# Attention block of a fused four-layer kernel: row pairs share tiles, the layer norm's scale and shift move to GpSimd, and the order of the row-pair loop is rewritten

## The chip, the core and the metric

The kernel runs on one core of one Trainium2 chip. The metric is device time in microseconds (us) from launch to the last output. Lower is better. All data are fp32.

An engine is named as the profile names it: PE is the matrix engine (TensorE), PEld its weight loads, DVE the vector engine, ACT the scalar engine, POOL is GpSimd, and SP is the engine that issues most of the transfers.

## The reference, cut to what matters

The input `x` is an image of 256 by 256 pixels with 128 channels. Four residual layers follow each other; the change touches layer 0 alone. Layer 0 normalises `x` by groups, then by a layer norm over the channels, and runs attention along each image row with a bias that all rows share:

```python
zn = (z - mu) * rsqrt(var + EPS) * ln_scale + ln_bias      # z: group-normalised x
q, k, v = (zn @ Wq), (zn @ Wk), (zn @ Wv)                  # 4 heads of 32 channels
bias = zn @ Wb                                             # one number per pixel and head
g = sigmoid(zn @ Wg)
scores = einsum('bijhd,bikhd->bijkh', q, k) / sqrt(32) + bias[:, None]
a = softmax(scores, axis=-2)                               # over the 256 columns k of row i
o = g * einsum('bijkh,bikhd->bijhd', a, v)
x = x + o @ Wo
```

The other three layers (a gated recurrence over a spectrum, a triangle product, a convolution) are the same in both kernels.

## The kernel before

Channels lie on the 128 partitions and pixels along the free axis. The whole program is unrolled. The stages run one after the other: `transpose_in` (the image is transposed to channel-major form and its group statistics are taken), then `attention`, `recurrence`, `triangle` and `convolution`. Each engine works through its own queue in order; a tile's readers and writers are tied by semaphores, and a pool hands out a fixed number of buffers per name, so that the next user of a buffer waits for the last reader of the one before. `pin` keeps the instructions in the order in which the code emits them.

**Weights.** `attention_weights` folds the layer norm's `ln_scale` into every projection matrix and its `ln_bias` into a bias column per projection (`wb["q"]`, `wb["k"]`, `wb["gn"]`, `vb` for v, `wb["4"]` for the pair bias). So the stored `zn` is the centred and scaled value alone, and each projection adds its bias where it is read out of PSUM. `bounded` computes a bound on the scores; if it is small enough, as in these runs, `attend_bounded` is taken, which needs no maximum in the softmax. Otherwise `attend_any` would be.

**Norm stage** (inside `attention`): 64 blocks of 1024 pixels. For each block PE centres the pixels (`zc`), ACT squares them (`sq`), DVE copies them out (`zs`), PE averages the squares (`var`), ACT takes a logarithm and an exponential (`rs`), and DVE multiplies (`zn`). `pair_bias` runs once per two blocks, two blocks late: PE multiplies `zn` by the bias weights (`pbias`), DVE copies the result out (`bi`), POOL's queue stores `zn` in DRAM (`znT`, L352), and SP's queue stores the bias.

**Attention loop** (`attend_bounded`, L620 to L646): 128 row pairs `rp`, with rows `a = 2 rp` and `b = 2 rp + 1`. The steps, with the names that the profile shows:

- `project` (two pairs ahead): PE makes q, k, v, g for 512 pixels (`ppq`, `ppk`, `ppv`, `ppg`). ACT reads q, k and g out, DVE reads v out (`tv`). These four and the output `px` share two PSUM buffers under the tag `pj`.
- `score` (one pair ahead): PE makes a row's scores for four heads (`sc`), two heads to a PSUM buffer, two buffers in all.
- `biased`: DVE adds the shared bias `bT` to two heads at once (`e`, 128 x 1024), and `exponent`: ACT takes the exponential in place.
- `fold`: DVE adds the two halves of the columns (`es`), so that the softmax's denominator needs half the matmuls.
- `values`: PE makes numerator and denominator of one row in one PSUM tile (`nd`, one bank, two buffers).
- `gated`: DVE multiplies the denominator by `1 + exp(-g)` (`dn`); `inverse`: ACT takes a logarithm and an exponential of it; `divide`: DVE multiplies the numerator by it (`og`).
- `output`: PE applies Wo (`px`), DVE adds the residual row (`x`); `squares`: ACT takes the statistics for the next layer (`junk`).

Instructions are issued through helpers, so the profile gives the helper's line: L60 for every matmul, L54 for an activation, L308 for the vector work of the norm stage, L477 for that of the attention loop. The tile names tell them apart.

The PSUM memory is full: four banks of `sc`, two of `pj`, two of `nd`.

Of the kernel before, what the change touches and what calls it, by code (L numbers as in the profile page):

```python
# [9 lines left out]
F32 = mybir.dt.float32  # L10
AF = mybir.ActivationFunctionType
# [6 lines left out]
P = 128  # L18
# [12 lines left out]
class Kernel:  # L31
# [186 lines left out]
    def attention_weights(self, wp):  # L218

        nc, tc, I = self.nc, self.tc, self.i  # L220
        with self.pool(name="awp", bufs=1, space=PSUM) as ps0:
            def load(src, name):
                t = wp.tile(list(src.shape), F32, name=name)
                nc.scalar.dma_start(t, src)
                return t
            lns, lnb = (load(I["L0_conv_ln_" + n].rearrange("(c o) -> c o", o=1), "ln" + n[0]) for n in ("scale", "bias"))
            w, wb, raws = {}, {}, {}

            for nm, f in (("q", -1.0 / math.sqrt(HD)), ("k", 1.0), ("v", 1.0), ("g", 1.0), ("b", -1.0)):
                raw = raws[nm] = load(I["L0_conv_W" + nm], "raw" + nm)  # L230
                m = raw.shape[1]
                pb = ps0.tile([P, 2], F32, name="pb" + nm, tag="gn")
                self.mm(pb[:m, 0:1], raw, lnb)
                wb[nm] = wp.tile([m, 1], F32, name="wb" + nm)
                nc.vector.tensor_scalar_mul(wb[nm], pb[:m, 0:1], 0.5 if nm == "g" else f)
                w[nm] = wp.tile([P, m], F32, name="w" + nm)
                nc.vector.tensor_scalar(w[nm], raw, lns, f, ALU.mult, ALU.mult)
            wb["gn"] = wp.tile([P, 1], F32, name="wbgn")
            nc.vector.tensor_scalar_mul(wb["gn"], wb["g"], -2.0)

            vbl = wp.tile([P, P], F32, name="vbl")
            nc.vector.tensor_copy(vbl, lnb.to_broadcast([P, P]))
            pvb = ps0.tile([P, P], F32, name="pvb", tag="gn")
            self.mm(pvb, vbl, raws["v"])
            vb = wp.tile([P, P], F32, name="vb")
            nc.vector.tensor_copy(vb, pvb)
            wo = {"f": load(I["L0_conv_Wo"], "wo"), "h": wp.tile([P, P], F32, name="woh")}
            nc.vector.tensor_scalar_mul(wo["h"], wo["f"], 0.5)
            self.lnb = lnb

            wb["4"] = wp.tile([P, 1], F32, name="wbb4")
            nc.vector.memset(wb["4"], 0.0)
            for k in range(4):
                nc.vector.tensor_copy(wb["4"][32 * k:32 * k + NH], wb["b"])
            w["32"] = wp.tile([P, 32], F32, name="wb32")
            nc.vector.memset(w["32"], 0.0)
            nc.vector.tensor_copy(w["32"][:, :NH], w["b"])
        return w, wb, vb, wo, self.bounded(wp, raws, w, wb)
# [21 lines left out]
    def attention(self, wp, weights, later, xT, x1T, znT, biasD, stats0, stats1, shift1):  # L280
        nc, tc, I = self.nc, self.tc, self.i
        w, wb, vb, wo, small = weights
        with ExitStack() as c:
# [18 lines left out]
            with ExitStack() as c1:  # L302
# [4 lines left out]
                wbb, wb32 = wb["4"], w["32"]  # L307
                pin = lambda f: lambda *a, **k: tc.keep_in_program_order(f(*a, **k))  # L308
                mm, act, tt, ts = pin(self.mm), pin(self.act), pin(V.tensor_tensor), pin(V.tensor_scalar_add)
                flat = lambda t: t.rearrange("p k n -> p (k n)")  # L310
# [23 lines left out]
                def normalise(b):  # L334
# [7 lines left out]
                    tt(zn[b // 2][:, s:s + 1024], zs[b], rs, ALU.mult)  # L342

                def pair_bias(m):
# [6 lines left out]
                    ts(bi, pb, wbb)  # L351
# [27 lines left out]
            with tc.If(flag > 0) as branch:  # L379
                self.attend_bounded(xT, x1T, znT, bias, first, w, wb, vb, wo, stats1, shift1)  # L380
            self.last = {}
            with branch.Else():
                self.attend_any(xT, x1T, znT, bias, w, wb, wo, stats1, shift1)
# [70 lines left out]
    def attend_bounded(self, xT, x1T, znT, bias, first, w, wb, vb, wo, stats1, shift1):  # L454
# [4 lines left out]
        with ExitStack() as c:  # L459
# [20 lines left out]
            loaded, t, e, es, nd, dn, og, x1s = {0: first}, {}, {}, {}, {}, {}, {}, {}  # L480
# [14 lines left out]
            def project(rp, nm):  # L495
# [4 lines left out]
                if nm == "v":  # L500
# [3 lines left out]
                    tt(o, pv, vb.unsqueeze(1).to_broadcast([P, 4, P]), ALU.add)  # L504
                else:
                    pp = ps.tile([P, 512], F32, name="pp" + nm, tag="pj")
                    mm(pp, w[nm], z)
                    if nm == "g":

                        act_t(o, pp, AF.Exp, bias=wb["gn"], scale=-1.0)  # L510
                    else:
                        act_i(o, pp, AF.Identity, bias=wb[nm])
# [16 lines left out]
            def biased(i, p2):  # L529
                if i < N:  # L530
                    x = hp.tile([P, 2, 2, N], F32, name="e", bufs=8)
                    tt(x, e[i, p2], bT[:, 2 * p2:2 * p2 + 2], ALU.add)
                    e[i, p2] = x

            def exponent(i, p2):
                if 0 <= i < N:
                    act_t(e[i, p2], e[i, p2], AF.Exp, scale=-1.0)

            def fold(i):

                x = es[i] = hp.tile([P, NH, N], F32, name="es")
                for p2 in range(2):
                    y = e[i, p2]
                    tt(x[:, 2 * p2:2 * p2 + 2], y[:, :, 0, :], y[:, :, 1, :], ALU.add)

            def values(i):

                v, r = t[i // 2, "v"], i % 2
                nd[i] = ps.tile([P, 2, N], F32, name="nd", tag="nd")
                for kc in range(2):  # L550
                    for h in range(NH):
                        hs = slice(h * HD, (h + 1) * HD)
                        mm(nd[i][hs, 0, :], v[:, 2 * r + kc, hs], e[i, h // 2][:, h % 2, kc, :], start=kc == 0, stop=kc == 1)
                folded = i in es
                for kc in range(1 if folded else 2):
                    for h in range(NH):
                        hs = slice(h * HD, (h + 1) * HD)
                        mm(nd[i][hs, 1, :], ones, es[i][:, h] if folded else e[i, h // 2][:, h % 2, kc, :],
                           start=kc == 0, stop=folded or kc == 1)

            def gated(i):

                d = dn[i] = hp.tile([P, N], F32, name="dn")
                g = t[i // 2, "g"][:, (i % 2) * N:(i % 2 + 1) * N]
                stt(d, g, 1.0, nd[i][:, 1, :], ALU.add, ALU.mult)

            def inverse(i):
                if i >= 0:
                    act_t(dn[i], dn[i], AF.Ln)
                    act_t(dn[i], dn[i], AF.Exp, scale=-1.0)  # L570

            def divide(i):
                if i < 0:
                    return
                if i % 2 == 0:
                    og[i // 2] = pj.tile([P, 512], F32, name="og")
                rows = slice((i % 2) * N, (i % 2 + 1) * N)
                tt(og[i // 2][:, rows], nd[i][:, 0, :], dn[i], ALU.mult)
# [27 lines left out]
            for h in range(NH):  # L606
                pt = ps.tile([P, 2, 2, P], F32, name="pbt", tag="nd")
                for jc in range(2):
                    for kc in range(2):
                        tc.keep_in_program_order(  # L610
                            nc.tensor.transpose(pt[:, kc, jc, :], bias[:, jc, h, kc * P:(kc + 1) * P], self.ident))
                tc.keep_in_program_order(
                    V.tensor_copy(bT[:, h].rearrange("p k j -> p (k j)"), pt.rearrange("p k a j -> p (k a j)")))
            for i in range(2):
                score(i)
                for p2 in range(2):
                    biased(i, p2)
                    if (i, p2) != (1, 1):
                        exponent(i, p2)
            for rp in range(N // 2):  # L620
                a, b = 2 * rp, 2 * rp + 1
                score(a + 2)
                inverse(b - 2)
                biased(a + 2, 0)
                divide(a - 2)
                biased(a + 2, 1)
                divide(b - 2)
                for nm in "qkvg":
                    if nm == "g":
                        fold(a)  # L630
                        exponent(b, 1)
                        exponent(a + 2, 0)
                    project(rp + 2, nm)
                output(rp - 1)
# [3 lines left out]
                fold(b)  # L638
                biased(b + 2, 0)
                exponent(b + 2, 0)  # L640
                biased(b + 2, 1)
                values(a)
                gated(a)
                inverse(a)
                values(b)
                gated(b)  # L646
            inverse(N - 1)
            divide(N - 2)
            divide(N - 1)
# [3 lines left out]
    def attend_any(self, xT, x1T, znT, bias, w, wb, wo, stats1, shift1):  # L653

        nc, tc = self.nc, self.tc
        with ExitStack() as c:
# [7 lines left out]
            with tc.For_i(0, N // 2) as rp:  # L664
# [5 lines left out]
                self.attend(rp, zn, xr, x1, w, wb, wo["h"], bias, pj, hp, ps, parts)  # L670
# [9 lines left out]
    def attend(self, rp, zn, xr, x1, w, wb, wo, bias, pj, hp, ps, stats1):  # L680
# [4 lines left out]
        for nm in ("q", "k", "g"):  # L685
# [3 lines left out]
            if nm == "q":  # L689
                self.act(t, pp, AF.Identity, bias=wb["q"])  # L690
            elif nm == "k":
                nc.vector.tensor_scalar_add(t, pp, wb["k"])
            else:

                self.act(t, pp, AF.Tanh, bias=wb["g"], scale=0.5)
# [41 lines left out]
        nc.vector.scalar_tensor_tensor(og, po.rearrange("c r j -> c (r j)"), wb["v"], proj["g"], ALU.add, ALU.mult)  # L737
# [714 lines left out]
```

## Time and profile before

| what | value |
|---|---|
| time, median of 3 runs | 5322.12 us (5320.36 to 5322.81) |
| the profiled execution's own time | 5321.36 us |
| its span, first to last instruction | 5319.6 us |
| mean granted clock of PE | 0.977 |
| PE busy | 5079.0 us (95%) |
| DVE busy | 4210.7 us (79%) |
| ACT busy | 3655.6 us (69%) |
| POOL busy | 266.7 us (5%) |

The busy times are sums over all stages. The stages that the change touches are short parts of the span: from 0 to about 232 us the image is transposed, from about 232 to 495 us the norm stage runs, from about 495 to 1835 us the attention loop. The profile tells when an instruction ran, how long it took, and what ended the idle time of its engine before it. Two instructions of DVE or ACT that follow each other without a wait overlap a little, so a row's mean duration is more than what one more instruction adds to the engine's time. Matmul durations are modelled and overlap as well; what PE needs is read from the start of one group of matmuls to the start of the next.

### The profile page before, as it was taken

How to read it: one execution, taken by the hardware profiler on the slowest of the kernel's cores; microseconds unless marked ns; L12 is line 12 of the kernel's file. 1: busy time of each engine (PE TensorE's matmuls, PEld its weight loads, DVE VectorE, ACT ScalarE, POOL GpSimd, SP SyncE). 2: the span in 40 equal slices, each digit the busy share in tenths (PEclk: the TensorE clock that was granted, in tenths of full speed). 3: DMA queues.
4: the chain of work that ended last, by engine and by line, in shares of the span. 5: the costliest groups of instructions: out<-in, count | busy, mean ns of one | idle time of the engine just before them, and what ended most of it. 6: DMA issues, size and time to landing. Idle time of an engine off the chain costs nothing.

```text
span 5319.6 us, 76896 instructions
## 1 busy us (share of the span) xinstructions
PE 5079.0 (95%) x30069; PEld 2836.1 (53%) x30069; DVE 4210.7 (79%) x5534; ACT 3655.6 (69%) x5179; POOL 266.7 (5%) x488
## 2 busy tenths in 40 slices
PE   6699999999999899999999999899999989999999
PEld 4433555555555433333333333338999954439999
DVE  5666999999999799999999999555333536679886
ACT  4376777777777799999999999684333357763110
POOL 1100000000000000000000000000111010000000
PEclk7799999999999999999999999999999999999999
DMA  8875222222222222222222221577667678865432
GB/s 282 339 265 199 72 80 76 80 76 77 80 73 83 71 63 68 69 69 69 68 73 69 65 72 65 230 284 263 232 231 243 233 270 301 291 221 181 149 125 68
DMA packets 185930, 788.66 MB, mean 148 GB/s; under 512 B 36083, under 2 KB 39432, under 8 KB 136384
## 3 DMA queue, kind: packets, MB, share of 16 engines
q1 hardware_dynamic: 120212, 514.73, 29.6%
q0 software_dynamic: 60416, 268.46, 13.0%
q8 instruction: 240, 3.93, 0.3%
q10 hardware_dynamic: 4936, 0.50, 0.1%
q14 instruction: 126, 1.03, 0.1%
HBM read 512.28 MB, written 271.32 MB: 147 GB/s over the span
## 4 chain that ended last, share of the span: by engine, by line
PE 52%; DVE 31%; issue 12%; ACT 2%; DMA 1%; POOL 1%; POOLq 0%; ACTq 0%; SPq 0%; DVEq 0%
PE z L60 9%; PE m L60 7%; PE nd L60 6%; PE sc L60 6%; PE po L60 4%; PE zc L60 3%; DVE tr L824 3%; DVE t L821 3%; DVE y L821 3%; DVE p L821 3%; DVE yf L821 3%; PE ppv L60 3%; PE ppq L60 3%; PE px L60 3%; PE ppk L60 2%
## 5 line engine op out<-in xcount | busy, mean ns | idle before, releaser
L54 ACT ACTIVATE e<-e 128x1024 f32<-128x1024 f32 x512 | 525.5, 1052 | 166.4 <-DVE e L477 166.3
L477 DVE TENSOR_TENSOR e<-sc,bT 128x1024 f32<-128x1024 f32 x512 | 612.3, 1217 | 25.1 <-PE sc L60 25.1
L984 DVE TENSOR_TENSOR LR<-z,sg 128x512 f32<-128x512 f32 x256 | 268.5, 1049 | 364.5 <-ACT sg L54 359.7
L60 PE MATMUL m<-U,v 128*128 128x128 f32 x4608 | 516.7, 276 | 6.6 <-DVE v L1299 6.6
L60 PEld LDWEIGHTS m<-U,v 128*128 128x128 f32 x4608 | 516.5, 192 | 6.7 <-DVE v L1299 6.7
L60 PE MATMUL z<-wf,zt 128*128 128x128 f32 x4096 | 460.7, 276 | 3.6 <-DVE zn L984 3.6
L60 PEld LDWEIGHTS z<-wf,zt 128*128 128x128 f32 x4096 | 460.6, 193 | 4.6 <-DVE zn L984 4.4
L60 PE MATMUL sc<-tq,tk 32*128 32x256 f32 x4096 | 361.4, 408 | 3.3 <-DVE e L477 3.3
L54 ACT ACTIVATE sg<-z 128x512 f32<-128x512 f32 x256 | 152.8, 597 | 307.8 <-PE z L60 307.8
L60 PE MATMUL var<-sq,omat 128*128 128x512 f32 x768 | 360.8, 599 | 1.2 <-ACT rs L54 1.2
L477 DVE TENSOR_TENSOR es<-e 128x512 f32<-128x512 f32 x512 | 329.1, 684 | 0.0
L54 ACT ACTIVATE rs<-var,eps 128x1024 f32<-128x1024 f32 x192 | 213.4, 1112 | 168.1 <-PE var L60 168.1
L60 PEld LDWEIGHTS sc<-tq,tk 32*128 32x128 f32 x4096 | 220.8, 184 | 190.6 <-issue 147.9
L54 ACT ACTIVATE dn<-dn 128x256 f32<-128x256 f32 (+1 forms) x640 | 279.8, 456 | 61.6 <-DVE dn L477 51.3
L60 PE MATMUL nd<-e,tv 128*32 128x256 f32 x4096 | 271.0, 382 | 0.0
L60 PE MATMUL zc<-xin,lc 128*128 128x512 f32 x512 | 247.5, 607 | 6.1 <-DVE zn L984 5.6
L60 PEld LDWEIGHTS var<-sq,omat 128*128 128x128 f32 x768 | 137.9, 189 | 203.7 <-issue 154.6
L60 PE MATMUL av<-y,ident 128*128 128x512 f32 x384 | 193.0, 612 | 44.0 <-DVE y L821 44.0
L60 PE MATMUL po<-LR 128*128 128x256 f32 x1024 | 222.2, 380 | 7.0 <-DVE LR L984 7.0
L1336 ACT COPY m4s<-m 128x512 f32<-128x512 f32 x32 | 18.7, 585 | 285.6 <-PE m L60 285.6
L60 PEld LDWEIGHTS po<-LR 128*128 128x128 f32 x1024 | 194.1, 190 | 34.2 <-DVE LR L984 7.7
L54 ACT ACTIVATE rs<-rs 128x1024 f32<-128x1024 f32 x192 | 202.8, 1056 | 6.1
(329 smaller groups left out, 10076.7 us busy)
## 6 DMA issues: line engine op xcount, KB each, us to landing
zt<-znT SPq DMA_DIRECT2D x128, 1024.0 KB
znT<-zn POOLq DMA_DIRECT2D x64, 1024.0 KB, 5.8
xin<-x2T SPq DMA_DIRECT2D x64, 1024.0 KB
xr<-x3T SPq DMA_DIRECT2D x46, 768.0 KB
xin<-in_x_dram SPq DMA_DIRECT2D x64, 512.0 KB
xT<-xo POOLq DMA_DIRECT2D x64, 512.0 KB, 10.2
xr<-xT SPq DMA_DIRECT2D x64, 512.0 KB
xin<-xT SPq DMA_DIRECT2D x32, 1024.0 KB
```

The lines of the kernel that those rows point to most:

```text
L54: return self.nc.scalar.activation(out, in_, func, bias=bias, scale=scale, **kw)
L60: return self.nc.tensor.matmul(out, lhsT, rhs, start=start, stop=stop)
L477: pin = lambda f: lambda *a, **k: tc.keep_in_program_order(f(*a, **k))
L821: pin(V.tensor_tensor(out, a, b_, op))
L824: pin(V.scalar_tensor_tensor(out, a, k, b_, op0, op1))
L984: pin = lambda f: lambda *a, **k: tc.keep_in_program_order(f(*a, **k))
L1336: nc.scalar.copy(m4, m[4])
```

## The change

It has four parts.

1. **Scale and shift.** The projections use the raw weights (q and the pair bias with their constant factors), and all bias columns are gone. In the norm stage a new POOL instruction, one for each block of 128 x 1024, multiplies `zn` in place by `ln_scale` and adds `ln_bias`. The read-outs of q, k and g lose their bias operand.
2. **v.** It is read out of PSUM by ACT in place of DVE.
3. **Shared tiles.** The biased scores and exponentials of a row's four heads lie in one tile of 128 x 2048 (`e`, four buffers in place of eight of half the size). `fold` is one instruction for each row in place of two (the folded tile is now called `ks`). Numerators and denominators of both rows lie in one PSUM tile of two banks (`nd`, one buffer in place of two of half the size). `gated`, `inverse` and `divide` run once for each pair on 128 x 512 in place of twice on 128 x 256.
4. **Order.** In each pass of the loop the folds of both rows follow the projections, the four exponentials of a pair are all issued in the pass that makes their scores, and `gated` ends the pass. The order on PE stays: scores of `a + 2`, q, k, v, g, output, scores of `b + 2`, numerators and denominators of both rows.

`attend_any` and `attend` are adapted to the weights; they do not run here.

```diff
@@ attention_weights
-            wb["gn"] = wp.tile([P, 1], F32, name="wbgn")
-            nc.vector.tensor_scalar_mul(wb["gn"], wb["g"], -2.0)
...
-            pvb = ps0.tile([P, P], F32, name="pvb", tag="gn")
-            self.mm(pvb, vbl, raws["v"])
...
+        small = self.bounded(wp, raws, w, wb)
+
+        for nm, f in (("q", -1.0 / math.sqrt(HD)), ("b", -1.0)):
+            nc.vector.tensor_scalar_mul(w[nm], raws[nm], f)
+        w.update((nm, raws[nm]) for nm in "kvg")
...
@@ normalise
-                    tt(zn[b // 2][:, s:s + 1024], zs[b], rs, ALU.mult)
+                    z = zn[b // 2][:, s:s + 1024]
+                    tt(z, zs[b], rs, ALU.mult)
+                    nc.gpsimd.tensor_scalar(z, z, lns, lnb, ALU.mult, ALU.add)
@@ pair_bias
-                    ts(bi, pb, wbb)
+                    copy(bi, pb)
@@ project
-                    tt(o, pv, vb.unsqueeze(1).to_broadcast([P, 4, P]), ALU.add)
+                    act_i(o, pv, AF.Identity)
...
-                        act_t(o, pp, AF.Exp, bias=wb["gn"], scale=-1.0)
+                        act_t(o, pp, AF.Exp, scale=-1.0)
                     else:
-                        act_i(o, pp, AF.Identity, bias=wb[nm])
+                        act_i(o, pp, AF.Identity)
@@ biased, exponent, fold
-                    x = hp.tile([P, 2, 2, N], F32, name="e", bufs=8)
-                    tt(x, e[i, p2], bT[:, 2 * p2:2 * p2 + 2], ALU.add)
-                    e[i, p2] = x
+                    if not p2:
+                        es[i] = hp.tile([P, NH, 2, N], F32, name="e", bufs=4)
+                    hs = slice(2 * p2, 2 * p2 + 2)
+                    tt(es[i][:, hs], e[i, p2], bT[:, hs], ALU.add)
...
+                    x = es[i][:, 2 * p2:2 * p2 + 2]
+                    act_t(x, x, AF.Exp, scale=-1.0)
...
-                for p2 in range(2):
-                    y = e[i, p2]
-                    tt(x[:, 2 * p2:2 * p2 + 2], y[:, :, 0, :], y[:, :, 1, :], ALU.add)
+                x = ks[i] = hp.tile([P, NH, N], F32, name="ks")
+                tt(x, es[i][:, :, 0], es[i][:, :, 1], ALU.add)
@@ values, gated, inverse, divide
-                nd[i] = ps.tile([P, 2, N], F32, name="nd", tag="nd")
+                nd[rp] = ps.tile([P, 2, 2, N], F32, name="nd", bufs=1)
...
-                d = dn[i] = hp.tile([P, N], F32, name="dn")
-                stt(d, g, 1.0, nd[i][:, 1, :], ALU.add, ALU.mult)
+                d = dn[rp] = hp.tile([P, 2, N], F32, name="dn")
+                stt(d, t[rp, "g"].rearrange("p (r n) -> p r n", r=2), 1.0, nd[rp][:, :, 1], ALU.add, ALU.mult)
...
-                tt(og[i // 2][:, rows], nd[i][:, 0, :], dn[i], ALU.mult)
+                    tt(og[rp].rearrange("p (r n) -> p r n", r=2), nd[rp][:, :, 0], dn[rp], ALU.mult)
@@ attend_bounded, before the loop
-                pt = ps.tile([P, 2, 2, P], F32, name="pbt", tag="nd")
+                pt = ps.tile([P, 2, 2, 2, P], F32, name="pbt", tag="sc")
@@ the loop
                 score(a + 2)
-                inverse(b - 2)
+                inverse(rp - 1)
                 biased(a + 2, 0)
-                divide(a - 2)
                 biased(a + 2, 1)
-                divide(b - 2)
+                divide(rp - 1)
                 for nm in "qkvg":
                     if nm == "g":
-                        fold(a)
-                        exponent(b, 1)
                         exponent(a + 2, 0)
                     project(rp + 2, nm)
+                fold(a)
+                fold(b)
                 output(rp - 1)
                 score(b + 2)
                 exponent(a + 2, 1)
                 squares(rp - 1)
-                fold(b)
-                biased(b + 2, 0)
-                exponent(b + 2, 0)
-                biased(b + 2, 1)
-                values(a)
-                gated(a)
-                inverse(a)
-                values(b)
-                gated(b)
+                for p2 in range(2):
+                    biased(b + 2, p2)
+                    exponent(b + 2, p2)
+                values(rp)
+                gated(rp)
```

## The prediction

> **What bounds the kernel now.** First the busy shares over time: the attention loop from 495 to 1835 us is the only large stage touched. So I took 103 us from its middle, ten passes:
>
> ```profile
> core 0: us, PE busy (x) PEld busy (x) DVE busy (x) ACT busy (x) POOL busy (x), PEclk, DMA share, GB/s
> 1000.00:1103.00 103.00, 103.00 (x964) 53.40 (x960) 97.41 (x151) 81.10 (x131) 2.66 (x5) 1.00 0.26 78
> ```
>
> A pass takes 10.30 us (the scores of `a + 2` start at 526.14 and, 125 passes later, at 1813.44). DVE is busy 9.74 of it, ACT 8.11. PE's modelled 100% says little, so the chain of waits, one pass of it:
>
> ```profile
> 1010.44 1.59 PE sc L60 x16
> 1012.03 1.06 PE ppq L60 x2
> 1013.09 0.86 PE ppk L60 x2
> 1013.94 1.08 PE ppv L60 x8
> 1015.02 0.86 PE ppg L60 x2
> 1015.88 1.05 PE px L60 x2
> 1016.93 1.08 PE sc L60 x16
> 1018.01 2.73 PE nd L60 x48
> ```
>
> The same `sc` work takes 1.59 us for row a and 1.08 for row b. `ppv` takes 1.08 where eight matmuls 0.112 apart need 0.90, `px` 1.05 where `ppk`, of the same shape, needs 0.86. The waits of that window name the causes:
>
> ```profile
> PEld px L60 <- DVE tv L477: 7.5, 10, 0.8
> PEld ppv L60 <- ACT tq L54: 7.5, 10, 0.8
> ...
> DVE tv L477 <- PE ppv L60: 3.6, 10, 0.4
> ...
> PEld sc L60 <- DVE e L477: 2.3, 10, 0.2
> DVE e L477 <- PE sc L60: 1.8, 10, 0.2
> ```
>
> (A PEld wait contains time in which the matmul before still runs; the sizes come from the chain.) PE waits for the `sc` buffer that DVE reads late, for `tq`, for `tv`. Without these PE needs 10.30 - 0.51 - 0.18 - 0.19 = **9.4 us**. DVE waits only 0.18 (`sc`) + 0.36 (`ppv`) a pass: **DVE bounds the loop, PE is 9% behind it.**
>
> In the norm stage PE is busy 260 of 263 us, two blocks take 8.06 us, and DVE waits for ACT there: PE bounds it.
>
> **What the Trainium skill says.** (1) "VectorE: DVE Perf Modes", the section on the TRN2 errata: a DVE instruction pays a fixed cost, and an fp32 tensor-tensor takes (N+151)/0.96 ns. The trace agrees: 1226 ns for `zn` (1024), 684 for `es` (512). So merging saves the fixed part alone. (2) "ScalarE: Activation LUTs", What ACT_TABLE_LOAD costs: a per-partition pointer operand adds about 93 ns. The trace agrees: 688 against 597 in these rows:
>
> ```profile
> L54 ACT ACTIVATE tq<-ppq,wbq 128x512 f32<-128x512 f32 x10 | 6.9, 688 | 3.0 <-PE ppq L60 3.0
> ```
>
> ```profile
> L54 ACT ACTIVATE sg<-z 128x512 f32<-128x512 f32 x256 | 152.8, 597 | 307.8 <-PE z L60 307.8
> ```
>
> (3) "SBUF — State Buffer", Who interferes with whom: a DVE instruction with two SBUF inputs and a GpSimd instruction that reads SBUF block each other. No row shows it.
>
> **The change, step by step.** What one more instruction adds is read from pairs:
>
> ```profile
> 1010.76 0.74 DVE L477 SCALAR_TENSOR_TENSOR dn<-tg,nd 128x256 f32<-128x256 f32 x2
> ...
> 1015.67 1.28 DVE L477 TENSOR_TENSOR es<-e 128x512 f32<-128x512 f32 x2
> ...
> 1018.79 2.35 DVE L477 TENSOR_TENSOR e<-sc,bT 128x1024 f32<-128x1024 f32 x2
> ```
>
> The second adds 0.74 - 0.41 = 0.33, 1.28 - 0.68 = 0.60, and 2.35 - 1.22 = 1.13 us, for 256, 512 and 1024 columns.
>
> *DVE, a pass:* `tv` leaves, -0.60. Folds: four of 0.60 become two of 1.13, -0.14. `dn`: two of 0.33 become one of 0.60, -0.06; `og` the same, -0.06. From 9.74 to 8.9.
>
> *ACT:* `tv` arrives, +0.60 (the `sg` row). Three bias operands go, -0.27. `dn`: four of 0.41 become two of 0.62, -0.39 (0.41 plus 256 columns at (1052-412)/768 = 0.83 ns). From 8.11 to 8.05.
>
> *PE:* the same matmuls in the same order, 9.4. Now PE is the longest. Whether it waits needs the new order. With 0 where the scores of `a + 2` start, in us:
>
> - PE starts: scores a 0, q 1.08, k 2.04, v 2.90, g 3.79, `px` 4.65, scores b 5.60, `nd` 6.68 to 9.40.
> - DVE: the last `gated` ends 0.8. `e` of a waits for the scores, 1.16 and 2.30 (ends 3.51); divide 3.43; folds 4.03 and 5.17 (ends 6.38); `x` 6.30; `e` of b 6.92 and 8.06 (ends 9.28); `gated` after `nd`.
> - ACT: logarithm 0.96 and exponential to 2.2, `tq` 2.24, `tk` 3.06, `tv` 3.95, exponential 4.55, `tg` 5.5, exponential 6.1, `junk` 7.05, exponentials 8.16 and 9.30 (ends 10.35, which is 0.95 of the next pass, where the logarithm waits for it).
>
> PE's waits and their slack: v for `tq` (2.84) 0.06; g for `tk` (3.66) 0.13; `px` for `tv` (4.55) 0.10 and `og` (4.1) 0.5; scores b for the reads of a (3.51) 2.1; `nd` for the folds (6.38) 0.3; the next scores a for the reads of b (9.28) 0.12. All are met, four by 0.13 or less. The single `nd` buffer is read out by 4.1 and written at 6.68: no cost, and it has 2.5 us of cover. Late next is PE itself. For the thin slacks I add 0.1: **a pass of 9.5**, bounds 9.4 (all met) and 9.9 (four slacks missed by 0.1 each). Gain 125 x 0.80 = **100 us** (50 to 112).
>
> *Norm stage.* One POOL multiply-add per block, behind `zn` and ahead of `pbias` and the store:
>
> ```profile
> 340.17 1.23 DVE L308 TENSOR_TENSOR zn<-zs,rs 128x1024 f32<-128x1024 f32 x1 [1.55 <-ACT rs L54]
> ...
> 341.69 0.53 POOL L352 DMA_DIRECT2D znT<-zn  x1 [7.53 <-DVE zn L308]
> ...
> 342.98 1.07 PE L60 MATMUL pbias<-zn,wb 128*32 128x512 f32 x8
> ```
>
> `zn` ends at 341.40, `pbias` starts at 342.98: 1.58 us of cover. POOL starts 0.29 after its release, so an operation of up to about X = 1.25 us is hidden. Beyond that `pbias` waits, `var` is queued behind it on PE, and the next `zn` hangs on that `var`: 32 pairs x (X - 1.25). The only POOL compute in the trace writes alone:
>
> ```profile
> L175 POOL MEMSET ka<- 21x2048 f32 x2 | 3.5, 1794 | 0.3 <-POOLq L1443 0.3
> ```
>
> At 0.88 ns a column that bounds X from below: 0.9 us. "GPSIMD Engine Reference", Elementwise — side-by-side cycle accounting, gives 1.03 cycles a column for light bodies, 1.8 for a tight loop, 2.6 with two inputs: estimates of 0.9, 1.5 and 2.2 us. I take 1.3: **+2 us** (0 to +31). The copy of `bi` keeps its cost. The port conflict stays away: the next `zn` multiply starts 2.2 us or more after the last ends. The store is queued behind the next block's operation, some 5 us later; its landing takes 5.8 us and the buffer is rewritten 18 us after `zn`, so 7 us remain.
>
> *Once:* the last block's operation stands before `pbias` and the loop, cover gone: +1.5. The drain after the last `nd` does two rows in single steps: +1. The weights' set-up loses about ten small instructions under a stage with DMA 89% busy: 0. Two 1024-column copies for four of 512 in the prologue: -0.1.
>
> Sum: 5321.4 (the profiled execution, 0.8 below the median) - 100 + 2 + 1.5 + 1 = **5226**. Forecast range 5210 to 5250.
>
> **Rivals.**
> A. *POOL is slow, X near 2.2 us.* +31 in the norm stage: 5226 + 29 + 1 = 5256. For it: two-input price. Against: one input.
> B. *The slacks fail.* ACT at 2.2 to 4.6 serves three PE buffers in a row; a delay of 0.2 at each makes a pass of 10.0: 125 x 0.3 = 38, so 5288. For: three engines within 1.4 us. Against: the queues catch up where slack is 2 us.
> C. *Slower: POOL's arithmetic is software so slow that it bounds the norm stage.* From X = 1.25 + 97/33 = 4.2 us it eats the whole gain; at 5 us the time is about 5349. For: no row prices it. Against: 4.7 times the MEMSET's.
> D. *The shared tile ties its halves.* If `e` of two heads had to wait for the exponential of the other two, each pass would have 1.1 us more on DVE: 10.3 to 10.4, and 5325 to 5340. Against: `zn` is shared so too, and `pbias` for its first half ran at 489.96 while the second half was written at 491.87.
>
> **How the numbers follow.** Forecast 0.63, A 0.14, B 0.11, C 0.05, D 0.07. The range 5205 to 5270 takes forecast and A. A difference of 0.2% (11 us) is about what a measurement of this kernel can tell from no change. Faster: forecast, A and B, 0.88; same: part of D, 0.03; slower: C and the rest of D, 0.09.
>
> **What would show it.** Right: passes of 9.4 to 9.6; in the chain `sc` of a near 1.08, `ppv` 0.9, `px` 0.86 to 0.95; DVE's waits now for `sc` and `nd`, 0.6 to 0.8 a pass; norm stage still 263 us. Wrong: PE waiting for `tv` or `tq` (B), `pbias` for POOL (A, C), `e` for ACT (D).

## The result, and the profile after

| | before | after |
|---|---|---|
| time, median | 5322.06 us (5320.36 to 5322.81, 4 runs) | 5238.95 us (5236.77 to 5240.01, 4 runs) |
| ratio to before, 95% interval | | 0.9844 (0.9827 to 0.9861) |
| profiled execution, own time; span | 5321.36; 5319.6 us | 5238.88; 5237.0 us |
| steady pass of the attention loop | 10.296 us | 9.593 us |
| steady pair of norm blocks | 8.06 us | 8.06 us |

The change saves 83 us. On the same chip as later experiments the changed kernel ran again: 5235.97 us, ratio 0.9844 (0.9827 to 0.986), pass 9.593.

Where the 82.6 us of span went, from the starts of the stages' first and last matmuls:

| stretch | difference, us |
|---|---|
| start to the first `pbias` | -1.9 |
| norm stage, first to last `pbias` | +2.8 |
| last `pbias` to the first scores | -1.5 |
| loop, first to last scores (a pass is 0.703 shorter) | -87.7 |
| last scores to `zd`, an early matmul of the recurrence | +2.8 |
| all later stages, whose code is unchanged | +2.9 |

The first stretch differs by 4 us between the two profiles of the changed kernel, so its -1.9 says nothing. From `zd` to the end the profiles show 3478 to 3482 us, with no tie to any part of the change. So the loop is the case, and its own view is ten-odd passes from its middle, first the busy times, then one pass of the chain of waits (start, duration, what):

```profile
core 0: us, PE busy (x) PEld busy (x) DVE busy (x) ACT busy (x) POOL busy (x), PEclk, DMA share, GB/s
1000.00:1103.00 103.00, 103.00 (x1049) 54.35 (x1047) 94.65 (x108) 89.65 (x130) 3.19 (x6) 1.00 0.27 85
```

```profile
1005.98 1.08 PE sc L60 x16
1007.05 1.05 PE ppq L60 x2
1008.11 0.86 PE ppk L60 x2
1008.97 0.99 PE ppv L60 x8
1009.96 0.86 PE ppg L60 x2
1010.82 0.95 PE px L60 x2
1011.77 1.08 PE sc L60 x16
1012.85 2.73 PE nd L60 x48
```

The scores of row a now take 1.08 us like those of row b; they took 1.59. That is 0.51 of the 0.70 us; `ppv` and `px` give 0.09 and 0.10. What is left above PE's own need is small and lies in two places: `ppv` at 0.99 and `px` at 0.95. The waits of the same window (in total, times, longest) say for what, and show DVE on the other side of the line:

```profile
PEld px L60 <- ACT tv L54: 7.2, 11, 0.7
PEld ppv L60 <- ACT tq L54: 6.6, 10, 0.7
...
DVE dn L471 <- PE nd L60: 4.5, 11, 0.4
...
DVE e L471 <- PE sc L60: 3.6, 10, 0.4
```

DVE now waits twice a pass for PE, 0.41 + 0.36 us. It has stopped being the bound; PE is.

### The profile page after: what moved, and what is told of

Its sections match the earlier page's. It is cut to its first block, busy times and chain, and to the rows that moved or that the text cites. A ratio compares the mean times of both kernels' runs of the same rounds, so it can differ in the third digit from the quotient of the medians.

```text
span 5237.0 us, 75959 instructions
## 1 busy us (share of the span) xinstructions
PE 4997.8 (95%) x30067; PEld 2805.6 (54%) x30067; DVE 4091.4 (78%) x4886; ACT 3684.9 (70%) x5051; POOL 344.4 (7%) x552
## 4 chain that ended last, share of the span: by engine, by line
issue 50%; PE 41%; DVE 5%; POOL 2%; DMA 1%; ACT 1%; POOLq 0%; ACTq 0%; DVEq 0%; SPq 0%
PE z L60 9%; PE m L60 7%; PE zc L60 4%; PE po L60 4%; PE nd L60 3%; PE sc L60 3%; PE var L60 2%; PE py L60 2%; DVE stats L966 1%; DVE x L966 1%; PE ppq L60 1%; PE ppv L60 1%; PE px L60 1%; PE ppk L60 1%; PE ppg L60 1%
## 5 line engine op out<-in xcount | busy, mean ns | idle before, releaser
L54 ACT ACTIVATE e<-e 128x1024 f32<-128x1024 f32 x512 | 540.3, 1055 | 64.1 <-DVE e L471 54.9
L60 PE MATMUL sc<-tq,tk 32*128 32x256 f32 x4096 | 299.0, 403 | 2.3 <-DVE e L471 1.4
L471 DVE TENSOR_TENSOR ks<-e 128x1024 f32<-128x1024 f32 x256 | 300.6, 1215 | 0.0
L60 PEld LDWEIGHTS sc<-tq,tk 32*128 32x128 f32 x4096 | 187.6, 185 | 160.3 <-issue 97.1
L54 ACT ACTIVATE dn<-dn 128x512 f32<-128x512 f32 x384 | 241.6, 629 | 12.7 <-DVE dn L471 1.9
```

Source lines behind the costliest of these rows:

```text
L54: return self.nc.scalar.activation(out, in_, func, bias=bias, scale=scale, **kw)
L60: return self.nc.tensor.matmul(out, lhsT, rhs, start=start, stop=stop)
```

## The experiments

The questions: which part of the change makes the pass short, what the last 0.19 us of a pass are, and what the POOL instruction costs. The theory from the prediction was that DVE's freed time is what counts, and that the thin slacks of PE's buffers take back a little. The rival was that the order alone decides, because the old one has DVE wait at a fixed place. Each edit is shown against the changed kernel, unless the text says otherwise. All times are medians of 4 runs; the ratios are to 7 runs of the kernel before on the same chip. Three chips were used, so runs are best compared by ratio or by pass.

| run | time, us | ratio (95%) | pass, us |
|---|---|---|---|
| e1: parts 1 and 2 alone | 5296.75 | 0.995 (0.9933 to 0.9966) | 10.108 |
| e3: all but the order | 5290.56 | 0.9938 (0.9921 to 0.9955) | 10.040 |
| e9: e3, and the fold of b ahead of the output | 5265.15 | 0.9894 (0.9877 to 0.991) | 9.800 |
| e2: all but v's move | 5281.75 | 0.9921 (0.9904 to 0.9938) | 9.958 |
| e4: bias operands back | 5247.48 | 0.9856 (0.984 to 0.9873) | 9.683 |
| e7: three `pj` buffers | 5211.98 | 0.9794 (0.9778 to 0.981) | 9.403 |
| e8: v in the denominators' bank | 5208.60 | 0.9788 (0.9771 to 0.9804) | 9.403 |
| e5: no POOL instruction | 5236.52 | 0.9842 (0.9826 to 0.9859) | 9.593 |
| e6: POOL instruction twice | 5271.56 | 0.9906 (0.989 to 0.9923) | 9.593 |

### e1: old tiles, old order

Scale and shift on POOL and v on ACT stay; tiles, folds and order are those of before.

```diff
-                    es[i] = hp.tile([P, NH, 2, N], F32, name="e", bufs=4)
+                    x = hp.tile([P, 2, 2, N], F32, name="e", bufs=8)
...
-                fold(a)
-                fold(b)
                 output(rp - 1)
...
+                fold(b)
```

> Only parts 1 and 2 of the change: scale and shift on POOL, no bias columns, v read out by ACT; tiles and order as before. If the loss of v's read-out from DVE carries the gain: DVE's chain of a pass is 10.30 less 0.60 (the read-out) less 0.36 (its wait) = 9.3 us, PE's waits make it 9.6 to 9.9 us a pass, 5235 to 5275 us. If the shared tiles and the new order carry it: 10.1 to 10.3 us a pass, 5300 to 5325 us.

Measured: 5296.75 us, a pass of 10.108. The main expectation missed and the rival was right (the time lies just below its range): 0.69 us of DVE's busy time left the pass (9.74 to 9.04), and it got only 0.19 us shorter. The chain shows that none of DVE's freed time reaches the scores of a, which still take 1.59 us; the 0.19 us are those of `ppv` and `px`, which wait for read-outs of ACT.

```profile
1009.78 1.59 PE sc L60 x16
...
1013.29 0.99 PE ppv L60 x8
...
1015.14 0.95 PE px L60 x2
```

DVE's timeline shows where its freed time is (start, duration, engine, line, operation; in brackets the idle time before and its releaser):

```profile
1013.96 1.28 DVE L471 TENSOR_TENSOR es<-e 128x512 f32<-128x512 f32 x2
1016.13 0.69 DVE L471 SCALAR_TENSOR_TENSOR x<-px,xr 128x512 f32<-128x512 f32 x1 [0.89 <-PE px L60]
1016.75 0.08 DVE L471 DVE_READ_ACCUMULATOR x<-px,xr 128x1 f32 x1
1016.75 1.29 DVE L471 TENSOR_TENSOR es<-e 128x512 f32<-128x512 f32 x2
```

DVE stands 0.89 us at `x`, which needs PE's `px`, with the folds of row b queued behind it. The folds need nothing of `px`. Behind them stand the reads of b's scores that free the buffer for the next scores of a. The freed time came out as idle time at the head of a queue.

### e3: new tiles, old order

Everything of the change except part 4.

```diff
                     if nm == "g":
+                        fold(a)
+                        exponent(b, 1)
                         exponent(a + 2, 0)
                     project(rp + 2, nm)
-                fold(a)
-                fold(b)
                 output(rp - 1)
                 score(b + 2)
                 exponent(a + 2, 1)
                 squares(rp - 1)
-                for p2 in range(2):
-                    biased(b + 2, p2)
-                    exponent(b + 2, p2)
+                fold(b)
+                biased(b + 2, 0)
+                exponent(b + 2, 0)
+                biased(b + 2, 1)
```

Row b's second exponential follows in the next pass, as in the order of before.

> The changed kernel with the old places of the folds and of row b's second exponential; tiles and engines as changed. If the order matters: DVE idles for px before x (0.5 us) and folds b after it, so row b's scores are read 0.4 us later than PE needs them: about 9.9 us a pass, 5260 to 5300 us. If the order is neutral: 9.6 us a pass, 5239 us.

Measured: 5290.56 us, within the expected times, with a longer pass than expected, 10.040. The shared tiles are worth 0.07 us a pass here, though they took 0.26 us of work off DVE; the wait at `x` has grown to 1.02 us:

```profile
1014.82 0.69 DVE L471 SCALAR_TENSOR_TENSOR x<-px,xr 128x512 f32<-128x512 f32 x1 [1.02 <-PE px L60]
```

### e9: the same, with one step moved

Against e3:

```diff
                     project(rp + 2, nm)
+                fold(b)
                 output(rp - 1)
...
-                fold(b)
```

> The new tiles in the old order (10.04 us a pass), with one step moved: fold of row b ahead of the output of the pair before, instead of behind it. The second exponential of row b stays put off into the next pass, as in the old order. Theory (what held the old order back is that DVE stood 1.0 us at x, waiting for px, with the fold of b queued behind it): the fold fills that wait, 0.6 to 1.1 us of it come free, and part of it shows: a pass of 9.65 to 9.85, 5248 to 5274. Rival (it is the put-off exponential, which makes fold and values of the next pass late): a pass of 10.0, 5285 to 5292. If fold of b, moved ahead, now waits itself for that exponential, the pass is not shorter either, and the trace shows DVE waiting for ACT at ks in place of PE at x.

Measured: 5265.15 us and 9.800 us, inside the theory's range. One moved instruction is worth 0.24 us a pass, about as much as parts 1 to 3 together bring in the old order (10.296 - 10.040 = 0.26). What remains up to 9.593 us is the other difference, the exponential that is put off:

```profile
1009.59 1.22 DVE L471 TENSOR_TENSOR ks<-e 128x1024 f32<-128x1024 f32 x1
1011.40 1.23 DVE L471 TENSOR_TENSOR ks<-e 128x1024 f32<-128x1024 f32 x1 [0.60 <-ACT e L54]
1012.55 0.69 DVE L471 SCALAR_TENSOR_TENSOR x<-px,xr 128x512 f32<-128x512 f32 x1
```

`x` waits for nothing now. The fold of b (the second `ks`) waits 0.60 us for ACT instead, which was expected only if the pass did not get shorter; it got shorter all the same, and the scores of a, which need DVE's reads of b, still take 1.28 us. DVE's own order is the same as in the changed kernel; only ACT's is not. So the new order's 0.45 us divide into 0.24 for the fold and 0.21 for ACT's exponential.

### e2: v read out by DVE

```diff
-                    act_i(o, pv, AF.Identity)
+                    pin(V.tensor_copy)(o, pv)
```

> The changed kernel with v read out by DVE again (a copy). If DVE's chain from the scores of a to the last read of b's scores is what PE runs against (it ended 0.12 us early in the forecast): 0.60 us more on it make a pass of 10.0 to 10.2 us, 5285 to 5315 us. If ACT is the tighter engine, the 0.60 us that it loses offset this: at most 9.7 us a pass, at most 5255 us.

Measured: 5281.75 us and 9.958 us, just below what was expected. In the new order v's move is worth 0.37 us a pass (9.958 - 9.593). With it undone the chain shows both of the old signs:

```profile
1006.19 1.34 PE sc L60 x14
...
1011.29 1.05 PE px L60 x2
```

The scores of a wait for DVE again (1.34), and `px` waits longer, for a `tv` that DVE reads late (1.05). These 0.26 and 0.10 us make up the 0.37. No run has the new order with the old tiles, so what the tiles are worth in the new order is not known.

### e4: bias operands on the read-outs of q, k and g

A column of zeros is the bias, so that these three instructions take the form that they had before.

```diff
-                        act_t(o, pp, AF.Exp, scale=-1.0)
+                        act_t(o, pp, AF.Exp, bias=zb, scale=-1.0)
...
-                        act_i(o, pp, AF.Identity)
+                        act_i(o, pp, AF.Identity, bias=zb)
```

> The changed kernel with a column of zeros as bias operand in the read-outs of q, k and g, so that each costs ACT 0.09 us more. If PE waits for the release of the two projection buffers: v starts 0.09 us later, and part of it again for the output: 9.7 to 9.8 us a pass, 5250 to 5265 us. If ACT has room there: 9.6 us a pass, 5239 us.

Measured: 5247.48 us and 9.683 us: the direction as expected, the size a little smaller. `tq` takes 687 ns in place of 597. ACT is idle for 1.2 us of a pass in the changed kernel (13.35 of 103 us), yet the pass is 0.09 us longer: the 0.09 us stand between `ppq` and the PSUM buffer that v wants, and `ppv` takes 1.08 us in place of 0.99. So removing the bias columns, which asked for the POOL instruction, paid at one place out of three.

### e7: a third buffer under the tag pj

Numerators and denominators lie in one bank for the pair, the denominator's matmuls overwriting the numerators, and the bank that comes free is a third `pj` buffer. This leaves the numerators out of the result; the instructions are all there.

```diff
-                    pp = ps.tile([P, 512], F32, name="pp" + nm, tag="pj")
+                    pp = ps.tile([P, 512], F32, name="pp" + nm, tag="pj", bufs=3)
...
-                nd[rp] = ps.tile([P, 2, 2, N], F32, name="nd", bufs=1)
+                nd[rp] = ps.tile([P, 2, 1, N], F32, name="nd", bufs=1)
```

> The changed kernel with three PSUM buffers for the projections and the output in place of two; the bank comes from the numerators, which the denominators overwrite (it leaves the numerators out of the result; instructions and sizes stay). If the 0.2 us that a pass takes over the forecast's PE sum of 9.4 us are weight loads held back by the release of these buffers: 9.40 to 9.45 us a pass, 5212 to 5222 us. If they belong to the change of shape of the matmuls: 9.60 us a pass, 5239 us.

Measured: 5211.98 us and 9.403 us, as expected. The 0.19 us are the two `pj` buffers. In the chain `ppv` and `px` are at what their matmuls need:

```profile
1016.05 0.89 PE ppv L60 x8
1016.94 0.86 PE ppg L60 x2
1017.80 0.86 PE px L60 x2
```

### e8: the same without leaving anything out

PSUM is full, but the denominators' bank stands empty from `gated` (early in a pass) until the denominators are written at its end, and v is projected in between. So v shares that bank, and q, k, g and `px` have the two `pj` buffers to themselves.

```diff
-                    pv = ps.tile([P, 4, P], F32, name="ppv", tag="pj")
+                    pv = ps.tile([P, 4, P], F32, name="ppv", tag="dv", bufs=1)
...
-                nd[rp] = ps.tile([P, 2, 2, N], F32, name="nd", bufs=1)
+                nd[rp] = ps.tile([P, 2, N], F32, name="nd", bufs=1)
+                de[rp] = ps.tile([P, 2, N], F32, name="de", tag="dv", bufs=1)
```

> The changed kernel with the full computation, the PSUM banks dealt out anew: the numerators of a pair get one bank, the denominators another, and v's projection shares the denominators' bank (read out by gated at 0.8 us of a pass, written by v from 2.9, by the denominators after 6.7). q, k, g and px have the two pj buffers to themselves, so v waits for no read-out of q, g for that of q instead of k, and px for that of k instead of v. Theory (release of the two pj buffers holds back the weight loads of v and px by 0.1 us each): in the chain ppv 0.89 and px 0.86, a pass of 9.40 instead of 9.59, so 24 us off 5238: 5208 to 5220, and both kernels are beaten. Rival (sharing the denominators' bank only exchanges one wait for another: v for gated, or the denominators for tv; or the 0.19 of the run with a third buffer came from its left-out bank): a pass of 9.55 to 9.65, 5230 to 5245.

Measured: 5208.60 us (5207.54 to 5210.13), 9.403 us a pass: faster than both kernels, 114 us below before and 30 below the change (27 below the change's second set of runs). The loop's share of the 30 is 24.3 us, as expected; most of the rest lies in the image stage and the later stages, which e8 does not touch and which vary by up to 6 and 4 us from profile to profile. That v only exchanges one wait for another, the rival, is out: `ppv` takes 0.89 us here, as in e7. The weight loads show how the wait for a `pj` buffer acts. In the changed kernel (the weight load's wait in brackets):

```profile
1008.15 0.60 ACT L54 ACTIVATE tq<-ppq 128x512 f32<-128x512 f32 x1
1008.80 0.97 PEld L60 LDWEIGHTS ppv<-rawv,zn 128*128 128x128 f32 x8 [0.66 <-ACT tq L54]
1008.81 1.15 PE L60 MATMUL ppv<-rawv,zn 128*128 128x128 f32 x8
```

and in e8:

```profile
1004.17 0.19 PEld L60 LDWEIGHTS ppv<-rawv,zn 128*128 128x128 f32 x1 [0.24 <-DVE e L471]
1004.60 1.05 PE L60 MATMUL ppv<-rawv,zn 128*128 128x128 f32 x8
```

In e8 the first load runs 0.43 us ahead of its matmul, beside the last matmul of k. In the changed kernel the wait for `tq` sits on that load, which starts 0.05 us after `tq` ends, when the matmul is due; the load of 0.19 us is no longer hidden, and 0.10 us of it shows: from the first matmul of v to the second it is 0.21 us in place of 0.11. "TensorE: Matmul & The Clock Gate", Part 2: What happens when you issue a matmul, says that PE pulls weight loads ahead of matmuls in flight; both traces agree, and show that a load whose buffer is not yet released stays behind.

### e5 and e6: POOL's instruction left out, and twice

e5 takes the instruction out, e6 issues it twice. The changed kernel itself ran again beside them, as after_again.

```diff
-                    nc.gpsimd.tensor_scalar(z, z, lns, lnb, ALU.mult, ALU.add)
```

```diff
                     nc.gpsimd.tensor_scalar(z, z, lns, lnb, ALU.mult, ALU.add)
+                    nc.gpsimd.tensor_scalar(z, z, lns, lnb, ALU.mult, ALU.add)
```

> The changed kernel once more, as a yardstick for the next three: 5239 us, 9.60 us a pass by both theories.

> The changed kernel without the POOL multiply-add (it leaves out the layer norm's scale and shift). If the operation (1.19 us measured) is hidden but for the last block: 1.4 us less, 5236 to 5239 us, two blocks in 8.06 us. If it costs by contention with DVE's multiply: 10 us less or more, about 5229 us.

> The changed kernel with the POOL multiply-add issued twice for each block (scale and shift applied twice), so X is about 2.4 us. If the cover ends at 1.25 us: 32 pairs of blocks times 1.15 us, and 1.2 us at the end: 38 us more, 5265 to 5285 us, two blocks in 9.2 us. If there is more cover than that: 5240 us, two blocks in 8.06 us.

Measured: e5 5236.52 us against 5235.97 of the changed kernel beside it, no difference that a run can tell; e6 5271.56 us, 35.6 more. The changed kernel's group of that instruction (busy, mean ns, idle before) and one block of its timeline:

```profile
L336 POOL TENSOR_SCALAR zn<-zn,lns,lnb 128x1024 f32<-128x1024 f32 x64 | 76.2, 1190 | 167.7 <-DVE zn L299 123.7 <-PE pbias L60 38.9 <-issue 5.1
```

```profile
338.31 1.22 DVE L299 TENSOR_TENSOR zn<-zs,rs 128x1024 f32<-128x1024 f32 x1 [1.55 <-ACT rs L54]
...
339.63 1.20 POOL L336 TENSOR_SCALAR zn<-zn,lns,lnb 128x1024 f32<-128x1024 f32 x1 [3.31 <-DVE zn L299]
...
341.12 1.06 PE L60 MATMUL pbias<-zn,wb 128*32 128x512 f32 x8
```

POOL starts 0.10 us after `zn` ends and finishes 0.29 us ahead of `pbias`. One instruction of 1.19 us is hidden; a second one is not: in e6 two blocks take 9.11 us in place of 8.06, and from the first to the last `pbias` it is 34.3 us more. There the loads of `pbias` for the second of the two blocks wait for the second instruction and start 0.05 us after it:

```profile
342.81 1.20 POOL L336 TENSOR_SCALAR zn<-zn,lns,lnb 128x1024 f32<-128x1024 f32 x1 [2.71 <-DVE zn L299]
344.11 1.20 POOL L337 TENSOR_SCALAR zn<-zn,lns,lnb 128x1024 f32<-128x1024 f32 x1
...
345.35 0.14 PEld L60 LDWEIGHTS pbias<-zn,wb 128*32 128x32 f32 x4 [0.92 <-POOL zn L337]
```

From the start of the first instruction to the end of the second it is 2.49 us on the mean, so the cover is 2.49 - 1.05 = 1.44 us. The changed kernel's own trace gives the same: 1.48 us from POOL's start to the loads of `pbias`, less 0.05. The prediction had 1.25. Only at the stage's end does the one instruction show: the last three groups of four `pbias` matmuls wait for POOL. The last two blocks' `pbias` starts 5.04 us after that of the two blocks before, and its second half 4.26 us after its first, against 3.62 and 3.19 before, and the stage takes 250.24 us. In e5, which lacks the instruction, it takes 247.35 like the 247.40 of before.

## Why the prediction was right, and where it was off

5226 was predicted, 5239 measured: the right sign and the right new bound, with 13 us less of gain. What lets DVE's freed time reach PE was not named in the forecast (third point). By its steps:

- **The bound moves from DVE to PE: right.** The scores of a fell from 1.59 to 1.08, and DVE waits 0.77 us a pass for `sc` and `nd` (predicted 0.6 to 0.8). PE's need of 9.4 us a pass, got by taking its waits off the old chain, holds: e7 and e8 take 9.403. DVE's work came out as forecast, 8.83 us for 8.9. ACT's did not: it rose from 8.11 to 8.34 us where 8.05 was forecast, which cost nothing here.
- **The allowance for thin slacks: the term that was mis-sized.** 0.1 us was added, 0.19 was needed; over 125 passes that is 12 of the 13 us. The slacks were counted up to the start of the matmul: v needs `tq` at 2.90, has it at 2.84, "met". The timetable was good: in the trace `tq` ends 0.06 us before v's first matmul. But the wait sits on the weight load, which in e8 starts 0.43 us ahead and is hidden, and here starts with the matmul and is not. So v, waiting for `tq`, and `px`, waiting for `tv`, lost 0.10 us each although `tq` and `tv` were in time for the matmul. How much of the lead is needed was not measured; the load of g, 0.11 us ahead in both kernels, costs g nothing that shows (0.86). The slacks of `ppg` for `tk` and of the next scores held, as the chain's 0.86 and 1.08 show.
- **The order: right in the sum, and more important than it was given credit for.** The prediction took DVE's and ACT's work off the pass and put the rest on a new timetable. It did not say that the shorter work without the new timetable is worth only 0.26 us (e3), and the first expectation for e1 shows that this was not understood then: the same sum gave 9.6 to 9.9 us for the old order, which took 10.108. In e1 the way from `px` over `x`, the folds of b and the reads of b's scores to the next scores of a sets the pass, not the sum of DVE's work. Of the 0.70 us the order gives 0.45, if it comes last; undoing v's move alone loses 0.37. The parts need each other and their shares do not add up.
- **POOL's instruction: right, slightly too dear.** 1.3 us was assumed, bounded by 0.9 and 2.2; it takes 1.19. The cover was put too small, at 1.25 for 1.44: POOL starts 0.10 us after `zn`, not the 0.29 read from an instruction that issues a transfer. So the +2 us are 0. Of "GPSIMD Engine Reference", Elementwise — side-by-side cycle accounting, neither the light body (estimate 0.9 us) nor the tight loop (1.5) fits; the measured value lies between.
- **Once only: too small.** The end of the norm stage costs 2.8 us, not 1.5, since `pbias` waits for POOL three times there instead of once. The loop's drain costs 2.8, not 1. e1, with the old tiles in the old order, drains in 19.5 us (before: 19.4), e3, with the new tiles in the old order, in 21.8 and the changed kernel in 22.2: most of it comes with the shared tiles. From the last `pbias` to the scores 1.5 us were gained, not 0.1; e1 gains 1.4 there, so it comes with parts 1 and 2 and not with the prologue's larger copies. What in them gives it was not taken apart. The 2.9 us in the later stages stay unexplained.
- **The rivals.** A and C needed POOL at 2.2 and 4.2 us. B was half a truth: its sign, PE waiting for `tq` and `tv`, did show, and two slacks failed, by 0.10 each, which is a third of its 0.6 above PE's need. Two of the sums are off: from a pass of 9.5 to B's 10.0 it is 125 x 0.5 = 62 us, not 38, and only with 62 does one come to 5288; and four misses of 0.1 above 9.4 make 9.8, not 9.9. D is out: two exponentials and two additions run on halves of one tile at the same time, ACT starting when the first half is written:

```profile
1012.88 2.36 DVE L471 TENSOR_TENSOR e<-sc,bT 128x1024 f32<-128x1024 f32 x2
...
1014.14 2.19 ACT L54 ACTIVATE e<-e 128x1024 f32<-128x1024 f32 x2 [0.37 <-DVE e L471]
```

## What to carry to other kernels

Here work taken off the busiest engine was gained only once its queue had something else to do in the place where it would otherwise wait (e1 against the whole change): look for the instruction that waits at the head (here `x` for `px`) with independent work queued behind it, and move that work ahead. When PE is the bound, count the slack of a PSUM buffer up to the weight load, not up to the matmul; and before asking for another buffer, look for one that is idle at that time of the loop, as the denominators' bank was for v. Give POOL work only after measuring its cover: here 1.44 us of cover hid an instruction of 1.19 in the steady stage, its end cost 2.8 us once, and of the 1.29 us that a second such instruction adds 1.05 were paid.

## What the runs showed of the hardware

- **POOL's multiply-add of 128 x 1024 fp32 with two per-partition operands takes 1.19 us** in place, against 1.22 us of DVE's multiplication of two tiles of that size.
- **POOL holds DVE up, but only in one of three DVE instructions here.** In e6 the second POOL instruction reaches into the next `zn`, which reads two SBUF tiles. The overlap and the length, from e6's timeline:

```profile
344.11 1.20 POOL L337 TENSOR_SCALAR zn<-zn,lns,lnb 128x1024 f32<-128x1024 f32 x1
...
344.98 1.39 DVE L299 TENSOR_TENSOR zn<-zs,rs 128x1024 f32<-128x1024 f32 x1 [1.07 <-POOL zn L336]
```

  33 of the 64 `zn` overlap with no POOL instruction and take 1.225 us. 28 overlap by 0.32 to 0.33 us and take 1.39 to 1.40; two by 0.38 and take 1.449; one by 0.61 and takes 1.677. Each is longer by its overlap less 0.15 us, and all 31 end 1.07 us after POOL's instruction: DVE was held until POOL was done. POOL's instruction keeps its 1.19 us. `zs` and `bi`, which read PSUM, overlap POOL for most of their length and keep their 1.28 and 0.68 us. "SBUF — State Buffer", Who interferes with whom, says the same; in the changed kernel no `zn` overlaps POOL, as predicted. In e6 the hold of 0.17 us is not on the way to the next `pbias`, which starts 4 us after the POOL instructions behind it: the lateness of POOL's end, 2.49 - 1.43 = 1.06 us, accounts for the 1.05 us of a pair by itself.
